# Two cross-attentions in one kernel: the image outputs of each pair's first batch move from TensorE to GpSimd, and a batch's text outputs are transposed through one PSUM tile

## The chip, the cores and the metric

The kernel runs on one core of a Trainium2 chip. The metric is the device time of one execution in microseconds (us). The engines that matter here are TensorE (matrix products and transposes, results in PSUM), VectorE, ScalarE, GpSimd and SyncE, whose queue issues nearly all of the DMAs. In the profile's lines they are called PE, DVE, ACT, POOL and SP; PEld is TensorE's loading of weights, which overlaps its products. Every engine takes its own instructions in order and waits on semaphores for the others. [...]

## The reference

Two cross-attention layers run one after the other on x (64 batches of 256 tokens and 320 channels, float32), both with 20 heads of 16 channels. Layer 0 attends to 77 context tokens (its image part is empty here). Layer 1 splits the context into 73 text tokens and 4 image tokens. What matters here is layer 1, per batch and head:

```
probs_t  = softmax(q . k_t * scale)                   # 256 x 73
text_out = probs_t . v_t
sem      = cosine(probs_t . text, image tokens)       # 256 x 4
probs_ip = softmax(q . k_ip * scale + 0.5 * sem) * spatial_mask
out      = (text_out + probs_ip . v_ip) @ W_out + b_out + x
```

The last product of the fourth line's weights, `probs_ip . v_ip`, has a contraction over only 4 image tokens for each head. This product, for 16 of the 20 heads and for one of the two batches of a pair, is what the change moves.

## The kernel before

**Pairs and steps.** Two batches form a pair p (32 pairs). A pair takes ten steps, numbered k = 0 to 9, and the main loop counts steps g = 10 p + k. In each step, layer 0 handles one unit (a batch's 128 tokens by 8 heads, as scores of 4 row groups by 2 heads) and layer 1 handles one unit of an earlier pair, 13 steps behind (`LAG`). Work that belongs to whole batches or pairs (queries, keys, values, projections, image attention) is spread over the steps by `fillers(k, p)`, which returns four lists: `first`, `second`, `third` and `begin`. Each list is run at a fixed place in the step, so the list decides where an operation stands in every engine's order.

**A step on the engines.** At its start, TensorE writes the layer-1 weighted sums of the unit before (L760, L766) and the scores of both layers (L646) into one PSUM tile `sc` of four banks. There is one such tile (`psc`, bufs=1), so the next step's L760 can start only when VectorE has read the scores (L664, L666) and the products (L777, L780), and ScalarE has copied the sums out (L1092, in `sums_out`). Before that, `begin` runs, and if `held["i"]` is set, the copies that `image_attend` returned are put on ScalarE's queue. After the scores, TensorE transposes layer 1's probabilities (`transposed(1)`: `tr` and `rtr`, L710 and L711), does the `first` fillers, transposes layer 0's probabilities, and then does `second`, `attend` and `third`. ScalarE copies the transposes to SBUF (L717, L718 for layer 1, L736, L737 for layer 0), exponentiates (L674, L677, L678) and evacuates the fillers. GpSimd normalizes layer 0's probabilities (`normalize`, tile `parts`, L697), which the next step's transposes need, and then does the GpSimd work of the fillers. A manual dependency (`keep_order`) holds the order of TensorE, ScalarE, VectorE and GpSimd as it was written down; SyncE's DMAs are in that order only in the beginning and are ordered by the scheduler after that.

**Buffers.** Tiles with the same tag share their buffers: a new tile of a tag with bufs=1 may be written only when the last reader of the tile before has finished. PSUM has two banks for transposes (`ptr`, tag `tr`) and two for all other fillers (`pms`, tag `ms`). A filler such as `value_rows` (L381, the projection of context rows to values; L382 is its copy) takes one `ms` bank and thus waits for the copy of what lay in it.

**The text and image path of layer 1, pair p-2 while pair p is at its steps.** `text_output` divides the sums by the softmax's denominator on GpSimd (`an` for 16 heads, `an_last` for the last 4 heads); it runs when a batch's last unit ends, in step 9 for the first batch (b = 0) and in step 4 for the second (b = 1). `text_transposed` turns `an` on TensorE in four transposes (L846), through two `tr` tiles, into `aT` (two copies L848): in step 0 for b = 0, in step 5 for b = 1. The image weights (`image_scores` to `image_weights`, tile `iw`) are ready on GpSimd at the start of steps 2 (b = 0) and 7 (b = 1). For the 16 heads, `image_transposed` turns the weights of both batches on TensorE in step 7 (four transposes L948, one copy L950), and `image_attend` multiplies them in step 8 with block-diagonal image values `vip` (four products L960: both batches, two halves of the channels) into two `ms` tiles `ipv`. ScalarE copies these into `ip_out` (two copies L970) and GpSimd adds `ip_out` to `aT` (L972). `vip` is loaded with 16 small DMAs a batch (`image_values`, L478) and masked on GpSimd in step 9 (`place_image_values`, L483). The last 4 heads were already done on GpSimd before the change: `last_image_outputs` multiplies and adds for each of the 4 image tokens (tile `ip_last`, L857, and `an_last`, L860), in step 4 for b = 0 and in step 7's `second` list for b = 1; its values `vlast` are one broadcast DMA a batch (L489). In step 8, `last_transposed` transposes `an_last` (L866), and in step 9 `project` does the output projection from `aT`.

For the last pair, `image_attend` adds from PSUM on VectorE instead of copying with ScalarE.

## Time and profile before

| what | value |
|---|---|
| time, median of 3 runs (range) | 2574.57 us (2571.29 to 2574.81) |
| the profiled execution's own time | 2574.26 us |
| its span in the profile | 2572.5 us, granted TensorE clock 0.997 |
| busy: PE, PEld, DVE, ACT, POOL | 2514.1, 2009.7, 1952.3, 1506.8, 1654.6 us |
| HBM traffic | 95.56 MB read, 33.91 MB written |
| `vip` loads (L478) | 1024 DMAs of 4.0 KB |
| `vlast` loads (L489) | 64 DMAs of 128.0 KB |
| a usual pair in the middle (timeline of PE) | 75.9 us for ten steps |
| the steps 0 to 9 of such a pair | 8.0, 7.7, 7.65, 9.3, 8.6, 6.4, 6.8, 6.9, 6.75, 7.8 us |

The profile's span leaves out 1.8 us of the profiled execution's own time. A step is counted here from the start of its L760 to the start of the next step's L760 in TensorE's timeline. The lengths repeat from pair to pair within a few hundredths of a microsecond, apart from six pairs in which one more block of value rows lengthens steps 6 and 8 to 8.6 and 8.9 us. The engines' busy shares are averages over steps that differ in what limits them, so the stages around the change have to be read in the timeline. In a timeline line, the first number is the start in us, the second the time until the merged group ends, and a bracket at the end gives the idle time of the engine before it and the instruction that released it. In the view by stretches, PEclk is the granted clock of TensorE as a share of full speed.

### The profile page before, as it was taken

Reading aid. Unit: us, or ns where it says so; the run is one execution under the profiler, and the core shown is the slowest. Engines: PE = TensorE matmul, PEld = TensorE weight load, DVE = VectorE, ACT = ScalarE, POOL = GpSimd, SP = SyncE. Lnnn points to the kernel's source line nnn. Section 1 sums busy time; section 2 is a strip of 40 time slices with the busy share of each in tenths; the row PEclk is TensorE's granted clock in tenths of the full one; section 3 lists DMA queues with packets and bytes.
Section 4 is the critical chain, followed back from the end, with each engine's and each line's share of the span. In section 5 each row is a group of like instructions: output and inputs, shape, how many; then the busy total and the mean of one; then the engine's idle time right before and its main releaser. Section 6 shows DMA issues by size and latency. Waiting matters only on the chain.

```text
span 2572.5 us, 74528 instructions
## 1 busy us (share of the span) xinstructions
PE 2514.1 (98%) x27178; PEld 2009.7 (78%) x27178; DVE 1952.3 (76%) x3609; ACT 1506.8 (59%) x3893; POOL 1654.6 (64%) x4026
## 2 busy tenths in 40 slices
PE   7999999999999999999999999999999999999998
PEld 6677878777787777788777787778787777787776
DVE  4578777878777778777877777877877777777764
ACT  3465665665665665666656566666566666566543
POOL 3466666676666676666666666666666666666653
PEclk9999999999999999999999999999999999999999
DMA  5212211121211121211121211121211121211000
GB/s 166 59 44 62 60 48 43 54 59 56 63 46 48 49 59 55 64 45 52 45 60 54 64 44 53 45 59 54 66 45 50 44 60 54 64 41 42 25 25 27
DMA packets 186405, 138.33 MB, mean 54 GB/s; under 512 B 81016, under 2 KB 164728, under 8 KB 186040
## 3 DMA queue, kind: packets, MB, share of 16 engines
q1 hardware_dynamic: 185176, 132.41, 18.1%
q8 instruction: 217, 3.56, 0.6%
q14 instruction: 148, 1.21, 0.2%
q10 hardware_dynamic: 864, 1.15, 0.1%
HBM read 95.56 MB, written 33.91 MB: 50 GB/s over the span
## 4 chain that ended last, share of the span: by engine, by line
PE 72%; DVE 15%; ACT 5%; DMA 2%; issue 2%; SPq 2%; POOL 2%; DVEq 0%; POOLq 0%; ACTq 0%
PE sc L760 11%; PE tr L710 9%; PE q_ps L537 8%; PE sc L646 6%; DVE w L666 5%; PE o_ps L537 4%; PE v_ps L381 4%; PE sc L766 4%; PE k_ps L336 4%; DVE mx L664 4%; PE pv L794 3%; PE q_ps L546 3%; DVE prod L777 2%; PE pv L799 2%; PE o_ps L621 2%
## 5 line engine op out<-in xcount | busy, mean ns | idle before, releaser
L664 DVE TENSOR_REDUCE mx<-sc 128x8 f32<-128x584 f32 (+1 forms) x640 | 495.4, 774 | 423.9 <-PE sc L646 423.8
L697 POOL TENSOR_TENSOR parts<-w,sm 128x512 f32<-128x512 f32 (+1 forms) x640 | 440.5, 710 | 371.1 <-DVE sm L693 165.7
L666 DVE TENSOR_TENSOR w<-sc,mx 128x616 f32<-128x616 f32 x640 | 511.8, 800 | 66.7 <-ACT kT L339 0.5
L710 PE MATMUL tr<-ident,parts 128*128 128x128 f32 x2560 | 408.6, 282 | 8.2 <-POOL parts L697 3.8
L717 ACT COPY pt<-tr 128x512 f32<-128x512 f32 x320 | 187.5, 586 | 341.7 <-PE tr L710 339.0
L760 PEld LDWEIGHTS sc<-gv,pt 64*128 64x128 f32 x5120 | 319.5, 187 | 77.0 <-ACT sums L1092 53.7
L710 PEld LDWEIGHTS tr<-ident,parts 128*128 128x128 f32 x2560 | 285.0, 141 | 116.2 <-issue 76.1
L760 PE MATMUL sc<-gv,pt 64*128 64x94 f32 x5120 | 353.1, 277 | 15.8 <-ACT sums L1092 10.7
L674 ACT ACTIVATE w<-w 128x616 f32<-128x616 f32 x320 | 231.0, 722 | 151.9 <-DVE w L666 143.0
L692 DVE TENSOR_REDUCE sm<-w 128x8 f32<-128x616 f32 x320 | 250.7, 784 | 13.9 <-ACT w L674 13.9
L646 PE MATMUL sc<-kbd,q 32*128 32x154 f32 x5120 | 248.1, 305 | 1.0 <-ACT q L591 1.0
L537 PE MATMUL q_ps<-x,wq 128*128 128x256 f32 x1024 | 232.4, 379 | 3.4 <-ACT kT L339 3.4
L537 PE MATMUL o_ps<-aT,wo 128*128 128x256 f32 x1024 | 232.7, 380 | 0.0
L1092 ACT COPY sums<-sc 128x168 f32<-128x168 f32 x320 | 96.5, 302 | 230.8 <-DVE prod L780 230.1
L1174 DVE TENSOR_REDUCE nrm<-prod 128x8 f32<-128x584 f32 x320 | 227.0, 709 | 0.4
L777 DVE TENSOR_TENSOR prod<-sc,parts 128x512 f32<-128x512 f32 x320 | 217.7, 680 | 4.0 <-PE sc L766 4.0
L537 PEld LDWEIGHTS q_ps<-x,wq 128*128 128x128 f32 x1024 | 189.3, 190 | 27.6 <-ACT kT L339 4.6
L537 PEld LDWEIGHTS o_ps<-aT,wo 128*128 128x128 f32 x1024 | 190.4, 191 | 23.5 <-issue 0.2
L677 ACT ACTIVATE parts<-w 128x512 f32<-128x512 f32 x320 | 207.8, 649 | 0.0
L646 PEld LDWEIGHTS sc<-kbd,q 32*128 32x128 f32 x5120 | 186.5, 186 | 5.9 <-issue 4.8
L736 ACT COPY pt<-tr 128x512 f32<-128x512 f32 x256 | 150.4, 587 | 62.6 <-PE tr L710 62.6
L381 PE MATMUL v_ps<-wv,cf 128*128 128x320 f32 (+1 forms) x624 | 182.1, 438 | 0.0
(147 smaller groups left out, 4791.0 us busy)
## 6 DMA issues: line engine op xcount, KB each, us to landing
vip<-vip_rows SPq DMA_DIRECT2D x1024, 4.0 KB
out_dram<-x SPq DMA_DIRECT2D x64, 256.0 KB
x<-in_x_dram SPq DMA_DIRECT2D x31, 512.0 KB
v_rows<-vs SPq DMA_DIRECT2D x38, 320.0 KB
vm<-v_rows SPq DMA_DIRECT2D x152, 80.0 KB
ct<-in_ctx_dram SPq DMA_DIRECT2D x32, 308.0 KB
cf<-in_ctx_dram SPq DMA_DIRECT2D x38, 256.0 KB
g_rest<-gram_rest SPq DMA_DIRECT2D x512, 0.5 KB
```

Source lines behind the costliest of these rows:

```text
L381: nc.tensor.matmul(ps[:n, :C], cfs[i][:, k, :n], wv[l][:, k, :], start=(k == 0), stop=(k == KE - 1))
L537: nc.tensor.matmul(ps[b][:, m, :], w[:, k, m * P : (m + 1) * P], main[:, k, b * S : (b + 1) * S], start=(k == 0 and m == 0), stop=False,)
L646: nc.tensor.matmul(ps[:, r, 2 * T * l : 2 * T * (l + 1)], q[rows, b, :] if part == 2 else q[rows, t0 : t0 + P], kbd[rows, part].rearrange( ...
L664: nc.vector.tensor_reduce(mx, sc[:, :, :, :nt], AX.X, ALU.max)
L666: nc.vector.tensor_tensor(w, sc, mx.unsqueeze(3).broadcast_to([P, 4, 2, T]), ALU.subtract)
L674: nc.scalar.activation(w, w, AF.Exp, scale=SCALE)
L692: nc.vector.tensor_reduce(sm, w, AX.X, ALU.add)
L697: nc.gpsimd.tensor_tensor(two[:, 8 * t0 : 8 * t1].rearrange("p (h t) -> p h t", h=8), w[:, :, t0:t1], sm.unsqueeze(2).broadcast_to([P, 8, ...
L710: nc.tensor.transpose(ps[:, i, :], flat[:, i * P : (i + 1) * P], ident)
L760: nc.tensor.matmul(ps[:, i % 2 * 2 + j, at : at + GV], pt[half_rows, i, :], gv[b][half_rows, part, i, :], start=start and i < 2, stop=False,)
L777: nc.vector.tensor_tensor(prod[:, :, :, :M], sm[:, :, :, :M], w[:, :4].rearrange("p (e a) j t -> p (a j) e t", e=2), ALU.mult)
L1174: nc.vector.tensor_reduce(eight(stats[q, b][2], u), prod, AX.X, ALU.add)
```

## The change

For the first batch of each pair (b = 0), the 16 heads' image outputs are no longer made on TensorE. `head_values` loads the 4 image tokens' values once, broadcast to 128 partitions (tile `vt`, 512 KB, one DMA). `head_products` multiplies them by the weights for one image token (128x512), and `head_sum` adds the result to `an[0]`; four of each are spread over GpSimd's steps 2 to 4. `image_values`, `place_image_values`, `image_transposed` and `image_attend` then handle only b = 1: two transposes and two products where there were four, and the GpSimd add covers 128x512 instead of 128x1024. `vip` is loaded in step 9 and masked in step 1 of the following pair's steps.

`text_transposed` uses one `tr` tile and one copy for a batch. Since `an[0]` now has to hold the image outputs first, b = 0 is transposed in step 6 (`second` list) instead of step 0, after b = 1, and `an` has two buffers. In step 6 the sums are copied out (`sums_out`) after layer 0's transposes are copied instead of before. `last_image_outputs` for b = 0 is split: two tokens in step 4 and two in step 5, where the load of b = 1's `vlast` follows.

All products of this kind (`head_products`, `last_image_outputs`) and the copy out of `ipv` now share the tag `ip_out`, which has one buffer; before, `last_image_outputs` had a tile of its own (`ip_last`). `iw`, `vip` and `iwT` become smaller or lose a buffer.

```diff
--- before.py
+++ after.py
@@ -469,11 +469,17 @@
             rest0[:n].rearrange("p (i g) -> p i g", g=4).unsqueeze(3).broadcast_to([n, 2, 4, D]), ALU.mult,
         )
 
+    def head_values(p):
+
+        r0 = 2 * p * NIP
+        v = vips[p, "heads"] = small.tile([P, NIP, 2 * P], F32, tag="vt", name=f"vt{p}", bufs=1)
+        nc.sync.dma_start(v, vip_rows[r0 : r0 + NIP, : 2 * P].unsqueeze(0).broadcast_to([P, NIP, 2 * P]))
+
     def image_values(p, b):
 
 
         n, r0 = HT * NIP, (2 * p + b) * NIP
-        vip = vips[p, b] = big.tile([n, 2 * P], F32, tag="vip", name=f"vip{p}_{b}", bufs=3)
+        vip = vips[p, b] = big.tile([n, 2 * P], F32, tag="vip", name=f"vip{p}_{b}", bufs=1)
         for h in range(HT):
             nc.sync.dma_start(vip[h * NIP : (h + 1) * NIP, :], vip_rows[r0 : r0 + NIP, : 2 * P])
 
@@ -827,33 +833,47 @@
         sums = stats[p, b][1]
         rec = small.tile([P, 2 * H], F32, tag="rec", name=f"rec{p}_{b}", bufs=2)
         nc.vector.reciprocal(rec, sums[:, :, NIP + D])
-        an = big.tile([P, 2, HT, D], F32, tag="an", name=f"an{p}_{b}", bufs=1)
+        an = big.tile([P, 2, HT, D], F32, tag="an", name=f"an{p}_{b}", bufs=2)
         if b == 0:
             lasts[p] = big.tile([P, 2, 2, H - HT, D], F32, tag="an_last", name=f"an_last{p}", bufs=1)
         by_head(an, lasts[p][:, :, b], sums[:, :, NIP : NIP + D], rec)
-        return an
+        ans[b] = an
+
+    ans = {}
+
+    def head_products(p, t):
+
+        full = [P, 2, HT, D]
+        prod = made["ip"] = big.tile(full, F32, tag="ip_out", name=f"ip{p}_{t}", bufs=1)
+        nc.gpsimd.tensor_tensor(
+            prod, vips[p, "heads"][:, t].rearrange("p (h d) -> p h d", d=D).unsqueeze(1).broadcast_to(full),
+            weights[p, 0][:, :, :, t].unsqueeze(3).broadcast_to(full), ALU.mult,
+        )
+
+    def head_sum():
+
+        nc.gpsimd.tensor_add(ans[0], ans[0], made["ip"])
 
     def text_transposed(p, b):
 
-        an = made["an"]
-        if b == 0:
+        an = ans[b]
+        if b == 1:
             aTs[1, p] = channels("aT1", f"aT1_{p}", 1)
-        main = aTs[1, p][0]
+        ps = ptr.tile([P, 2, 2, P], F32, tag="tr", name=f"atr{p}_{b}")
         for s in range(2):
-            ps = ptr.tile([P, 4, P], F32, tag="tr", name=f"atr{p}_{b}{s}")
             t = an[:, s].rearrange("p h d -> p (h d)")
             for i in range(2):
-                nc.tensor.transpose(ps[:, i, :], t[:, i * P : (i + 1) * P], ident)
-            t0 = b * S + s * P
-            nc.scalar.copy(main[:, :, t0 : t0 + P], ps[:, :2])
-
-    def last_image_outputs(p, b):
+                nc.tensor.transpose(ps[:, i, s, :], t[:, i * P : (i + 1) * P], ident)
+        nc.scalar.copy(aTs[1, p][0][:, :, b * S : (b + 1) * S], ps.rearrange("p i s t -> p i (s t)"))
+
+    def last_image_outputs(p, b, tokens=range(NIP)):
 
         v = vips[p, b, "last"].rearrange("p t (h d) -> p t h d", d=D)
         w, to = weights[p, b, "last"], lasts[p][:, :, b]
         part = [P, 2, H - HT, D]
-        for t in range(NIP):
-            prod = small.tile(part, F32, tag="ip_last", name=f"ip_last{p}_{b}{t}", bufs=1)
+        for t in tokens:
+            prod = big.tile([P, 2 * S], F32, tag="ip_out", name=f"ip_last{p}_{b}{t}", bufs=1)
+            prod = prod[:, : 2 * HALF].rearrange("p (s h d) -> p s h d", s=2, d=D)
             nc.gpsimd.tensor_tensor(
                 prod, v[:, t].unsqueeze(1).broadcast_to(part), w[:, :, :, t].unsqueeze(3).broadcast_to(part), ALU.mult
             )
@@ -931,7 +951,7 @@
         nc.vector.tensor_reduce(r, num, AX.X, ALU.add)
         nc.vector.reciprocal(r, r)
         nc.gpsimd.tensor_mul(m, m, smask.unsqueeze(2).broadcast_to([P, 2, H]))
-        to = weights[p, b] = small.tile([P, 2, HT, NIP], F32, tag="iw", name=f"iw{p}_{b}", bufs=2)
+        to = weights[p, b] = small.tile([P, 2, HT, NIP], F32, tag="iw", name=f"iw{p}_{b}", bufs=1)
         last = weights[p, b, "last"] = small.tile(
             [P, 2, H - HT, NIP], F32, tag="iw_last", name=f"iw_last{p}_{b}", bufs=1
         )
@@ -942,36 +962,31 @@
     def image_transposed(p):
         n = HT * NIP
         ps = ptr.tile([P, 4, P], F32, tag="tr", name=f"itr{p}")
-        for b in range(2):
-            w = weights[p, b].rearrange("p s h t -> p s (h t)")
-            for s in range(2):
-                nc.tensor.transpose(ps[:n, 2 * b + s, :], w[:, s], ident)
-        wT = big.tile([n, S2], F32, tag="iwT", name=f"iwT{p}", bufs=1)
-        nc.scalar.copy(wT, ps[:n].rearrange("p j t -> p (j t)"))
+        w = weights[p, 1].rearrange("p s h t -> p s (h t)")
+        for s in range(2):
+            nc.tensor.transpose(ps[:n, s, :], w[:, s], ident)
+        wT = big.tile([n, S], F32, tag="iwT", name=f"iwT{p}", bufs=1)
+        nc.scalar.copy(wT, ps[:n, :2].rearrange("p s t -> p (s t)"))
         return wT
 
     def image_attend(p):
 
         wT = made["wT"]
-        both = [pms.tile([P, 512], F32, tag="ms", name=f"ipv{p}_{i}") for i in range(2)]
-        for b in range(2):
-            for i in range(2):
-                rows = slice(i * QR, (i + 1) * QR)
-                nc.tensor.matmul(
-                    both[i][:, b * S : (b + 1) * S], vips[p, b][rows, i * P : (i + 1) * P],
-                    wT[rows, b * S : (b + 1) * S], start=True, stop=True,
-                )
+        both = [pms.tile([P, 512], F32, tag="ms", name=f"ipv{p}_{i}")[:, :S] for i in range(2)]
+        for i in range(2):
+            rows = slice(i * QR, (i + 1) * QR)
+            nc.tensor.matmul(both[i], vips[p, 1][rows, i * P : (i + 1) * P], wT[rows, :], start=True, stop=True)
 
         def out_of(i):
-            main = aTs[1, p][0]
+            main = aTs[1, p][0][:, :, S:]
             if p == NP - 1:
-                nc.vector.tensor_add(main[:, i, :], both[i], main[:, i, :])
+                nc.vector.tensor_add(main[:, i], both[i], main[:, i])
                 return
             nc.scalar.copy(t[:, i, :], both[i])
             if i:
                 nc.gpsimd.tensor_add(main, t, main)
 
-        t = big.tile([P, 2, S2], F32, tag="ip_out", name=f"ip_out{p}", bufs=1)
+        t = big.tile([P, 2, S], F32, tag="ip_out", name=f"ip_out{p}", bufs=1)
         return [lambda i=i: out_of(i) for i in range(2)]
 
 
@@ -993,7 +1008,6 @@
                 add(1, p, values, 0, p, 0)
             add(0, p - 1, gram, p - 1, 0)
             add(0, p - 3, project_last, 1, p - 3)
-            add(2, p - 2, text_transposed, p - 2, 0)
             if p:
                 add(2, p, place_values, 0, p, 0)
             add(2, p - 1, values, 1, p - 1, 0)
@@ -1004,7 +1018,9 @@
                 add(1, p, place_values, 0, p, 0)
             add(0, p - 1, project, 0, p - 1)
             add(1, p - 2, last_image_values, p - 2, 0)
+            add(1, p - 2, head_values, p - 2)
             add(1, p - 1, place_gram, 0)
+            add(2, p - 2, place_image_values, p - 2, 1)
             add(1, p, keys_by_head, 0, p, 1)
             add(1, p - 1, keys_by_head, 1, p - 1, 0)
         elif k == 2:
@@ -1017,6 +1033,7 @@
             add(2, p - 1, lambda: made["q"]())
             add(1, p - 1, place_values, 1, p - 1, 0)
             add(1, p, values, 0, p, 1)
+            add(2, p - 2, head_products, p - 2, 1)
         elif k == 3:
             add(0, p + 1, load_context, p + 1)
             add(0, p, lambda: last_queries(0, p)())
@@ -1025,13 +1042,18 @@
             add(1, p - 1, queries, 1, p - 1)
             add(1, p, place_values, 0, p, 1)
             add(1, p - 1, keys_by_head, 1, p - 1, 1)
+            add(1, p - 2, head_sum)
+            add(1, p - 2, head_products, p - 2, 2)
+            add(1, p - 2, head_sum)
+            add(1, p - 2, head_products, p - 2, 3)
         elif k == 4:
             if p == 0:
                 add(0, p, image_keys, 1)
             else:
                 add(0, p, keys, 1, p, 0)
             add(1, p - 1, values, 1, p - 1, 1)
-            add(1, p - 2, last_image_outputs, p - 2, 0)
+            add(1, p - 2, head_sum)
+            add(1, p - 2, last_image_outputs, p - 2, 0, range(2))
             add(1, p + 1, queries, 0, p + 1)
         elif k == 5:
             if p == 0:
@@ -1039,7 +1061,8 @@
             add(0, p + 1, keys, 0, p + 1, 0)
             add(1, p - 1, gram, p - 1, 1)
             add(2, p - 2, text_transposed, p - 2, 1)
-            add(1, p - 2, last_image_values, p - 2, 1)
+            add(2, p - 2, last_image_outputs, p - 2, 0, range(2, NIP))
+            add(2, p - 2, last_image_values, p - 2, 1)
         elif k == 6:
             while len(made_rows) * P < min(NB, 2 * (p + 2)) * T:
                 rows_todo.extend((len(made_rows), l) for l in range(2))
@@ -1051,12 +1074,12 @@
             else:
                 add(1, p, keys, 1, p, 1)
             add(1, p, place_image_keys, p)
+            add(2, p - 2, text_transposed, p - 2, 0)
         elif k == 7:
             add(0, p + 1, keys, 0, p + 1, 1)
             add(1, p + 1, last_keys, p + 1)
             add(1, p - 2, lambda: made.update(wT=image_transposed(p - 2)))
             add(1, p - 2, last_image_outputs, p - 2, 1)
-            add(1, p - 1, image_values, p - 1, 0)
             if p == 0:
                 add(1, p, image_rows)
         elif k == 8:
@@ -1064,15 +1087,13 @@
                 add(0, p, value_rows, *rows_todo.pop(0))
             add(1, p - 1, place_gram, 1)
             add(1, p + 1, keys_by_head, 0, p + 1, 0)
-            add(1, p - 1, image_values, p - 1, 1)
             add(1, p - 1, place_values, 1, p - 1, 1)
             add(1, p - 2, last_transposed, p - 2)
             add(3, p - 2, lambda: held.update(i=lambda: image_attend(p - 2)))
         else:
             add(0, p - 2, project, 1, p - 2)
             add(1, p + 1, values, 0, p + 1, 0)
-            for b in range(2):
-                add(1, p - 1, place_image_values, p - 1, b)
+            add(1, p - 1, image_values, p - 1, 1)
         return f
 
     rows_todo, made_rows = [], [0, 1]
@@ -1148,7 +1169,7 @@
         if k != 2:
             for fn, args in first:
                 fn(*args)
-        if before1 and k in (1, 6, 8):
+        if before1 and k in (1, 8):
             sums_out(ps)
         if last0:
             transposed(0, *last0)
@@ -1161,7 +1182,7 @@
             keep_busy(8)
         if now[0] and k == 5:
             exponential(0, g, *now[0])
-        if before1 and k not in (1, 6, 8):
+        if before1 and k not in (1, 8):
             sums_out(ps)
         if now[1]:
             exponential(1, g, *now[1])
@@ -1174,11 +1195,13 @@
             nc.vector.tensor_reduce(eight(stats[q, b][2], u), prod, AX.X, ALU.add)
             if ends:
                 image_squares(q, b)
-                made["an"] = text_output(q, b)
+                text_output(q, b)
                 later[g + 1] = [(image_scores, (q, b))]
                 middle[g + 2] = (image_shifted, (q, b))
                 later[g + 2] = [(image_exponential, (q, b))]
                 early[g + 3] = [(image_weights, (q, b))]
+                if b == 0:
+                    early[g + 3] += [(head_products, (q, 0)), (head_sum, ())]
         for fn, args in second:
             fn(*args)
         if last0:
```

## The prediction

> **What bounds the kernel now.** I read the page first, then TensorE's timeline for step lengths, then the step that changes most (step 8) engine by engine, and last the view by stretches for the granted clock.

> ```profile
> span 2572.5 us, 74528 instructions
> PE 2514.1 (98%) x27178; PEld 2009.7 (78%) x27178; DVE 1952.3 (76%) x3609; ACT 1506.8 (59%) x3893; POOL 1654.6 (64%) x4026
> ```

> TensorE has almost no idle time, GpSimd has a third of its time free. That invites moving work from the one to the other, but averages do not tell what ends step 8. This is TensorE in step 8 of a usual pair (start 1281.05, next step 1287.80):

> ```profile
> 1281.05 1.13 PE L760 MATMUL sc<-gv,pt 64*128 64x94 f32 x16
> 1282.97 1.03 PE L960 MATMUL ipv<-iwT,vip 32*128 32x256 f32 x8
> 1283.93 0.66 PE L710 MATMUL tr<-ident,parts 128*128 128x128 f32 x4
> 1284.66 2.42 PE L381 MATMUL v_ps<-wv,cf 128*128 128x320 f32 x8
> 1286.92 0.60 PE L710 MATMUL tr<-ident,parts 128*128 128x128 f32 x4
> 1287.80 0.46 PE L760 MATMUL sc<-gv,pt 64*128 64x94 f32 x4
> ```

> ScalarE (first three lines) and GpSimd (last three) in the same step:

> ```profile
> 1284.03 1.07 ACT L970 COPY ip_out<-ipv 128x512 f32<-128x512 f32 x2 [1.39 <-PE ipv L960]
> 1287.12 0.43 ACT L382 COPY vs<-v_ps 128x320 f32<-128x320 f32 x1 [0.75 <-PE v_ps L381]
> 1287.45 0.30 ACT L1092 COPY sums<-sc 128x168 f32<-128x168 f32 x1
> ...
> 1281.39 1.38 POOL L697 TENSOR_TENSOR parts<-w,sm 128x512 f32<-128x512 f32 x2 [1.57 <-ACT parts L678]
> 1286.29 0.46 POOL L860 TENSOR_TENSOR an_last<-an_last,ip_last 128x128 f32<-128x128 f32 x1
> 1286.70 2.37 POOL L972 TENSOR_TENSOR aT<-ip_out,aT 128x1024 f32<-128x1024 f32 x1
> ```

> The reader should see a chain: the first ipv copy (start 2.98 us into the step) frees a PSUM bank, v_ps starts at 3.61, ends near 6.0, its copy L382 and the sums behind it on ScalarE end at 6.70, and the next step starts at 6.75. The view of line L970 confirms the first link:

> ```profile
> L970 ACT COPY ip_out<-ipv x62: 586/590/595, 210.0 to 2508.1; 128x512 f32<-128x512 f32 x62
>   PEld v_ps L381: 6.1, 29
> ```

> In 29 pairs v_ps waits for that copy already. Meanwhile GpSimd is still busy with the last four heads of b = 1: its last add ends 5.70 us into step 8, and I find 5.69 to 6.00 in all these 29 pairs.

> **The change part by part.** Times are for one pair, line numbers are of the kernel before.

> *The new wait (step 8).* The products of `last_image_outputs` for b = 1 and the tile that ScalarE copies ipv into now share one `ip_out` buffer. So the first ipv copy has to wait until GpSimd's last L860 has read its product. GpSimd cannot be earlier: its work in step 8 starts behind `parts` (L697), which waits for VectorE's sums of step 7. Step 7 gets shorter by 0.26 (below), so the last add ends 5.96 into step 8; with 0.02 of hand-over the copy starts at 5.98 instead of 2.98. It is shorter: 128x256, for which the copy L818 takes 0.37 where L970 takes 0.59. v_ps then starts at 5.98 + 0.37 + 0.04 = 6.39 instead of 3.61, 2.78 later. Behind the waiting copy on ScalarE's queue stand the second ipv copy, both copies of layer 1's transposes, layer 0's exponential, L382 and the sums; TensorE waits for the bank (v_ps) and then for the sums. All that follows v_ps keeps its distance, 3.18 to the next step, so step 8 grows by 2.78 to 9.5 us. The 0.43 us that half of ipv saves (four of eight records, 0.85 in the chain of waits) falls into this wait and is worth nothing.

> *Step 7, two transposes fewer.* Four L948 take 0.51 in the chain of waits, so 0.25 to 0.26 go. TensorE ends step 7 (sums are ready 0.44 before), so this counts in full: -0.26.

> *Steps 0 and 6, the text of b = 0.* Four transposes L846 take 0.59 in the chain. Step 0 is ended by TensorE, with the sums ready 0.8 earlier (1226.97 against 1227.78): -0.57. Step 6 now ends with TensorE waiting for the sums: the last filler's products are through at about 1273.7, the next L760 starts at 1274.17. So of 0.63 (with a gap) only some 0.15 shows: +0.15. In the six pairs whose step 6 carries one more block of value rows there is no such slack: +0.6. Copying the sums after layer 0's transposes costs nothing: those transposes end at 1272.84, their two copies take 0.86, and VectorE's product that releases the sums ends at 1273.78. If they came later, at most that 0.86 would be added.

> *GpSimd's new work.* A 128x512 product with a broadcast operand takes 1.05 (L697). For the add, the rows are 0.457 for 128x128 (L860) and 2.367 for 128x1024 (L972); their straight line gives 1.27 for 128x512. Four of each are 9.3 us, plus 0.08 between dependent ones, 9.9; with half of L972 for the add (1.18) it is 9.5, with twice L884's 0.63 for 128x256 for the product 10.8. One mask L483 (0.62) and half of L972 (1.1) go. Net +8 us of 76, GpSimd busy about 1900 us. Its cover is the idle time in steps 2 to 5: 4.43 before `least` (L897, step 4) takes four operations (4.7 us from 1254.5 to 1259.4, so L897 is about 0.5 late, and VectorE's L901 starts only at 1260.13 anyway); 2.14 before L921 in step 6 takes two tokens of `last_image_outputs` (2.0). `parts` of step 2 is late by 0.5 and of step 4 by 0.3, but the transposes that read them start 2.1 and 3.6 after `parts` ends now. So nothing; if each operation took twice as long, `parts` of step 4 would be 5.0 late and 1.4 us a pair would show.

> *Queues.* SyncE issues 16 small loads fewer, at 0.33 each (three in 0.97), and one 512 KB load more. This one waits for the last product of the pair before (step 4); behind it are the context load for a later pair and `gram`'s copies, which are ready only in step 5, so its wait delays nothing. Its data are first read some 60 us later. `vlast` of b = 1 is issued after the second split half, about 10 us before it is read. In step 3 the value loads stood behind up to fifteen `vip` loads, and four pairs lost 0.2 to 3.0 us in step 4 behind late values (4.4 in all): between 0 and -4.4, I take -2.

> *Sum with a full clock.* 2.78 - 0.26 - 0.57 + 0.15 = 2.10 in 23 pairs, 2.55 in six: 48.3 + 15.3 = 63.6. The last pairs have no v_ps; they gain a little (fewer transposes, shorter copies, some -1). Together 63.6 - 1 - 2 = +61, on the profiled execution's 2574.3 (0.3 below the median): 2635 us.

> *The clock.* TensorE would stand idle for 3.1 us in step 8, from 3.2 to 6.39, after the sparse score products. The trace shows what this can do. Here one idle time of 1.39 us (2412.0 to 2413.4) lies in the first stretch, and the last two lines are around one of 2.72 us (1950.15 to 1952.87), before and after which there are dense 128x128 products:

> ```profile
> 2411.70:2415.10 3.40, 2.02 (x39) 1.00 0.00 0
> 2415.10:2418.50 3.40, 2.65 (x21) 0.50 0.00 0
> 2418.50:2421.90 3.40, 3.40 (x28) 0.50 0.04 9
> 2421.90:2425.30 3.40, 3.40 (x52) 0.99 0.15 34
> ...
> 1950.90:1954.30 3.40, 1.43 (x7) 1.00 0.26 64
> 1954.30:1957.70 3.40, 3.40 (x52) 1.00 0.12 25
> ```

> After the short idle the clock was 0.50 for two stretches of 3.4 us and that step took 9.95 where others take 6.42: 1.75 lost per stretch. After 1.60 us at 2490 one stretch was at 0.50, after 3.31 at 2553 two. Five others in the trace (1.49 to 2.72) left it at 1.00. An idle time of 3.1 among sparse products is nearest to those that dropped, and what follows at half speed (v_ps) ends the step. I take one such stretch, 1.7 us, in three pairs of four: 29 x 0.75 x 1.7 = +37, bounds 0 and two stretches nearly everywhere (+89). So 2635 + 37 = 2672, rounded to 2670.

> [...]

> **The rivals.**
> - *The wait isn't there or is met in time.* It decides if GpSimd's last L860 ended by 2.6 us into step 8 instead of 5.96. Then step 8 loses some 0.2 (the sums end 6.5 into it), a usual pair -0.26 - 0.57 + 0.15 - 0.2 = -0.88, six pairs -0.43: -23, with the ends and loads 2548. For it: idle GpSimd elsewhere. Against it: its order is fixed and 5.69 is the earliest of the 29 ends.
> - *The wait, but the clock holds.* 2635, up to 2655 where few pairs drop. For it: 2.72 idle at 1.00. Against it: 1.39 idle dropping.
> - *The wait, and two slow stretches in most pairs.* 2635 + 89 = 2724. For it: two of three drops lasted two stretches. Against it: v_ps and the projection of step 9 are dense and should bring the clock back after one.
> - *GpSimd becomes the bound in steps 2 to 5.* Only with operations twice as long: +1.4 x 29 = +41 more. No row of GpSimd's elementwise work is so slow; I leave it to the tail.

> **How the numbers follow.** Wait with dropped clock, 2655 to 2708: 0.58. Wait with a clock that mostly holds, 2628 to 2655: 0.24. Above 2708: 0.08. Faster: 0.08. Within 0.2% (5 us, what a measurement of this kernel can tell from no change): 0.02. The range 2628 to 2708 holds 0.82. Slower is 0.58 + 0.24 + 0.08 = 0.90.

> **What would show it.** In the profile after: the first ipv copy idles some 3.4 us longer per pair for GpSimd's `an_last` add, about 90 us in sum; v_ps is preceded by 3.1 us of TensorE idle; step 8 takes 9.5 us or more and steps 7 and 0 about 6.6 and 7.45; step 6 stays near 6.95. GpSimd near 1900 us busy, ScalarE about 30 less than before. The clock row shows stretches at 0.50 around step 8, or the mean stays at 1.00, which decides between 2635 and more. The prediction is wrong if the ipv copy starts near 3 us into step 8, or if `parts` comes after the transposes that read it in steps 3 to 5.

## The result, and the profile after

| | time, median (range), us | span, us | granted clock |
|---|---|---|---|
| before (with the runs beside the changed kernel) | 2573.2 (2571.29 to 2574.81) | 2572.5 | 0.997 |
| changed | 2686.34 (2682.82 to 2689.27) | 2687.5 | 0.976 |

The changed kernel takes 1.0439 of the time before, 95% interval [1.0426, 1.0451]: it is 113 us slower. The prediction said 2670 (2628 to 2708), 96 us above the profiled execution of the kernel before.

The first fence shows lines of the page of the changed kernel: the engines' busy time, the chain that ended last, and the group of v_ps products (busy time and mean ns of one, then idle time before them and its releaser). Its last line is the same group in the page of the kernel before.

```profile
span 2687.5 us, 73637 instructions
PE 2535.9 (94%) x26986; PEld 2021.2 (75%) x26986; DVE 1959.1 (73%) x3609; ACT 1485.1 (55%) x3829; POOL 1893.8 (70%) x4250
...
PE 61%; DVE 12%; POOL 10%; ACT 5%; DMA 5%; issue 4%; SPq 3%; DVEq 0%; POOLq 0%; ACTq 0%
...
L381 PE MATMUL v_ps<-wv,cf 128*128 128x320 f32 (+1 forms) x624 | 220.4, 509 | 89.4 <-ACT ip_out L985 89.4
...
L381 PE MATMUL v_ps<-wv,cf 128*128 128x320 f32 (+1 forms) x624 | 182.1, 438 | 0.0
```

TensorE has fewer instructions than before and is busy for longer: 2535.9 against 2514.1 us. The v_ps group shows both reasons in one line. It now has 89.4 us of idle time in front of it (before: none), and the same 624 products take 220.4 us (before: 182.1), because some of them run at a lower clock (0.59 in one stretch of the second fence below). GpSimd's share of the chain that ends last was 2% and is 10%.

Step 8 of a usual pair (start 2068.81, next step 2079.87) in the timeline of TensorE, ScalarE and GpSimd:

```profile
2068.81 1.13 PE L766 MATMUL sc<-gv,pt 64*128 64x94 f32 x16
2070.72 0.60 PE L978 MATMUL ipv<-iwT,vip 32*128 32x256 f32 x4
2075.10 4.06 PE L381 MATMUL v_ps<-wv,cf 128*128 128x320 f32 x8 [3.08 <-ACT ip_out L985]
2078.99 0.60 PE L716 MATMUL tr<-ident,parts 128*128 128x128 f32 x4
...
2074.67 0.65 ACT L985 COPY ip_out<-ipv 128x256 f32<-128x256 f32 x2 [4.33 <-POOL an_last L880]
2075.21 0.60 ACT L723 COPY pt<-tr 128x512 f32<-128x512 f32 x1
...
2074.19 0.45 POOL L880 TENSOR_TENSOR an_last<-an_last,ip_last 128x128 f32<-128x128 f32 x1
2075.40 1.27 POOL L987 TENSOR_TENSOR aT<-ip_out,aT 128x512 f32<-128x512 f32 x1 [0.76 <-ACT ip_out L985]
```

The products ipv end at 2071.3, but their copy starts only at 2074.67, when GpSimd's last `an_last` add (L880, which has read the last product in the shared buffer) is through. TensorE then stands idle for 3.08 us, and its eight v_ps products take 4.06 us where 2.42 is normal. The view by stretches around the same place (stretch, its length, busy time of PE, PEld, DVE, ACT, POOL, then PEclk, DMA share, GB/s) says why:

```profile
2068.80:2071.90 3.10, 3.10 (x53) 2.55 (x49) 1.75 (x5) 1.49 (x6) 2.44 (x5) 1.00 0.13 30
2071.90:2075.10 3.20, 0.12 (x3) 0.00 (x1) 2.98 (x5) 0.43 (x2) 2.35 (x6) 0.99 0.00 0
2075.10:2079.20 4.10, 4.10 (x10) 2.72 (x11) 1.62 (x3) 1.50 (x5) 2.79 (x5) 0.59 0.16 38
2079.20:2083.00 3.80, 3.80 (x55) 3.31 (x54) 0.87 (x2) 2.59 (x8) 3.67 (x13) 1.00 0.48 160
```

The clock falls from 0.99 to 0.59 behind the idle time, in the stretch in which the work that ends the step is being done, and is at 1.00 in the next. In the view of waits (total us, number of times, longest) the new wait and a second loss can be read:

```profile
ACT ip_out L985 <- POOL an_last L880: 134.4, 31, 4.7
...
PE v_ps L381 <- ACT ip_out L985: 89.4, 29, 3.1
...
ACT nrm L925 <- DVE nrm L921: 13.9, 7, 2.7
...
PE k_ps L336 <- ACT q L597: 10.3, 6, 2.2
```

The last two are not among the waits that the profile of before lists. They belong to step 5, which became long in six pairs. In step lengths (means from TensorE's timeline, in us; a row runs from step 5 of a pair to step 4 of the next, and the means are over rows 2 to 28, counted from 0, which are called pairs below):

| step | 5 | 6 | 7 | 8 | 9 | 0 | 1 | 2 | 3 | 4 |
|---|---|---|---|---|---|---|---|---|---|---|
| before | 6.42 | 7.21 | 6.88 | 7.23 | 7.82 | 7.99 | 7.69 | 7.65 | 9.29 | 8.74 |
| changed | 7.12 | 7.33 | 6.73 | 11.45 | 7.82 | 7.27 | 7.69 | 7.61 | 9.29 | 8.67 |

Over 29 pairs these differences make 122 us in step 8, 20 in step 5, 3.5 in step 6, and -21 in step 0, -4 in step 7, -3 in steps 2 and 4: 117 us, for spans that differ by 115.

### The profile page after: what moved, and what is told of

Same layout as the page of the kernel before. It is cut to its first block, busy times and chain, and to the rows that moved or that the text cites. A ratio compares the mean times of both kernels' runs of the same rounds, so it can differ in the third digit from the quotient of the medians.

```text
span 2687.5 us, 73637 instructions
## 1 busy us (share of the span) xinstructions
PE 2535.9 (94%) x26986; PEld 2021.2 (75%) x26986; DVE 1959.1 (73%) x3609; ACT 1485.1 (55%) x3829; POOL 1893.8 (70%) x4250
## 3 DMA queue, kind: packets, MB, share of 16 engines
q14 instruction: 144, 1.18, 0.2%
## 4 chain that ended last, share of the span: by engine, by line
PE 61%; DVE 12%; POOL 10%; ACT 5%; DMA 5%; issue 4%; SPq 3%; DVEq 0%; POOLq 0%; ACTq 0%
PE sc L766 9%; PE v_ps L381 8%; PE tr L716 7%; PE q_ps L543 7%; PE sc L652 5%; PE o_ps L543 4%; DVE w L672 4%; PE k_ps L336 3%; DVE mx L670 3%; PE sc L772 3%; POOL an_last L880 2%; PE q_ps L552 2%; POOL ip_last L877 2%; PE pv L800 2%; DVE prod L783 2%
## 5 line engine op out<-in xcount | busy, mean ns | idle before, releaser
L723 ACT COPY pt<-tr 128x512 f32<-128x512 f32 x320 | 187.6, 586 | 358.0 <-PE tr L716 356.4
L381 PE MATMUL v_ps<-wv,cf 128*128 128x320 f32 (+1 forms) x624 | 220.4, 509 | 89.4 <-ACT ip_out L985 89.4
L381 PEld LDWEIGHTS v_ps<-wv,cf 128*128 128x128 f32 (+1 forms) x624 | 131.8, 220 | 150.9 <-ACT ip_out L985 96.3
```

The costliest lines, as they stand in the source:

```text
L381: nc.tensor.matmul(ps[:n, :C], cfs[i][:, k, :n], wv[l][:, k, :], start=(k == 0), stop=(k == KE - 1))
```

## The experiments

Two theories stood against each other at first. One: the shared buffer makes ScalarE's copy wait, and that wait with the clock behind it is the whole of step 8. The other: GpSimd has too much work, and the buffer only shows it. All ratios below are against the kernel before, run beside the experiment.

| run | time, us | ratio to before, 95% |
|---|---|---|
| own_tile | 2554.83 | 0.9923 [0.9907, 0.9940] |
| lend_before | 2682.56 | 1.0422 [1.0402, 1.0442] |
| fill_wait | 2648.82 | 1.0292 [1.0276, 1.0307] |
| lend_two | 2577.75 | 1.0020 [1.0011, 1.0030] |
| lend_three | 2639.19 | 1.0252 [1.0235, 1.0269] |
| early_products | 2589.54 | 1.0059 [1.0038, 1.0080] |
| own_heads_first | 2541.72 | 0.9873 [0.9858, 0.9887] |
| one_more_product | 2570.18 | 0.9989 [0.9980, 0.9999] |
| least_on_vector | 2599.71 | 1.0103 [1.0086, 1.0120] |
| one_more_least | 2600.34 | 1.0104 [1.0088, 1.0119] |
| least_late | 2543.26 | 0.9881 [0.9864, 0.9897] |
| two_banks | 2540.08 | 0.9869 [0.9855, 0.9884] |

### The buffer taken out of the change, and put alone into the kernel before

own_tile, an edit of the changed kernel:

```diff
-            prod = big.tile([P, 2 * S], F32, tag="ip_out", name=f"ip_last{p}_{b}{t}", bufs=1)
-            prod = prod[:, : 2 * HALF].rearrange("p (s h d) -> p s h d", s=2, d=D)
+            prod = small.tile(part, F32, tag="ip_last", name=f"ip_last{p}_{b}{t}", bufs=1)
```

> The changed kernel, only that the products of the last heads have a small tile of their own again (ip_last, 128x128) instead of the buffer that the copy of ipv waits for. Theory (the shared buffer): the copy ipv starts some 3.0 us into step 8 again, v_ps at about 3.6, no half-speed stretch there, step 8 about 6.5 instead of 11.4 on average: 29 x 4.9 = 142 us less, about 2545, of which the longer step 5 of six pairs (about 19 us above the step's usual length) may or may not be part: 2540 to 2562, faster than before by 0.4% or more. Rival 1 (GpSimd's added work is the cause, the buffer only shows it): step 8 stays above 8.5 and the time above 2630. Rival 2 (the wait goes elsewhere: the add to aT, the next transposes or the load of vt is late next): step 8 is 6.5, another step takes at least 1 us more in most pairs, 2575 to 2610.

lend_before, an edit of the kernel before:

```diff
-            prod = small.tile(part, F32, tag="ip_last", name=f"ip_last{p}_{b}{t}", bufs=1)
+            prod = big.tile([P, 2 * S2], F32, tag="ip_out", name=f"ip_last{p}_{b}{t}", bufs=1)[:, : 2 * HALF].rearrange("p (s h d) -> p s h d", s=2, d=D)
```

> The kernel before, only that the products of the last heads are made in the buffer ip_out, as the changed kernel has it; no other work is moved. Theory (the shared buffer alone makes the loss): the copy ipv waits for the last sum of GpSimd, v_ps starts about 2.8 us later, step 8 grows from 6.9 to 9.4 with the clock held and to 11 to 12 with one or two half-speed stretches: 2573 + 29 x (2.6 to 5) = 2648 to 2718, about 2690. Rival (the buffer costs only because GpSimd carries the head products too): under 2610.

With its own tile, the changed kernel takes 2554.83 us, 131.5 less than with the shared buffer and 0.8% less than the kernel before. Its step 8 in the timeline of TensorE, ScalarE and GpSimd:

```profile
1969.17 0.60 PE L978 MATMUL ipv<-iwT,vip 32*128 32x256 f32 x4
1970.30 2.34 PE L381 MATMUL v_ps<-wv,cf 128*128 128x320 f32 x8
...
1973.85 1.13 PE L766 MATMUL sc<-gv,pt 64*128 64x94 f32 x16 [0.26 <-ACT sums L1113]
...
1969.79 0.65 ACT L985 COPY ip_out<-ipv 128x256 f32<-128x256 f32 x2 [1.01 <-PE ipv L978]
...
1972.64 0.46 POOL L880 TENSOR_TENSOR an_last<-an_last,ip_last 128x128 f32<-128x128 f32 x1
1973.06 1.27 POOL L987 TENSOR_TENSOR aT<-ip_out,aT 128x512 f32<-128x512 f32 x1
```

GpSimd ends its last add 5.85 us into the step, as late as before the edit (5.83). The copy does not care any more: it starts at 2.54, v_ps follows at 3.05 without idle time, and step 8 takes 6.59 us in a usual pair. So GpSimd's load is not what makes step 8 long.

The kernel before with nothing but the shared buffer takes 2682.56 us, nearly as much as the changed kernel, though none of the new GpSimd work is in it. Its waits:

```profile
ACT ip_out L970 <- POOL an_last L860: 124.6, 30, 4.7
...
PE v_ps L381 <- ACT ip_out L970: 79.0, 29, 3.0
```

Both runs came out within their theory's numbers. The buffer alone accounts for the loss in step 8, in either kernel. This is shown by putting it in and by taking it out.

### The wait without the half clock

fill_wait, an edit of the changed kernel in `transposed`; the added transposes write columns that nothing reads:

```diff
         nc.tensor.transpose(pr[:n, 0, :], flat[:, 4 * P : 4 * P + n], ident)
+        if l and now[0] and g % NU == 8:
+            for i in range(22):
+                nc.tensor.transpose(pr[:, 1 + i % 3, :], ident, ident)
```

> The changed kernel with the wait left in, but 22 more transposes of the identity behind the transposes of step 8, into columns of their bank that nothing reads, so that TensorE works about 3 us of the wait. Theory (the wait itself is some 2.8 us and the rest of step 8 is the halved clock): v_ps starts where it did, lasts 2.4 instead of 4.06, step 8 is 9.4 to 9.6 in all pairs, granted clock back near 0.995, time 2686 - 29 x 2.0 = about 2628 (2615 to 2640). Rival (the lengthening behind the wait is the queue of ScalarE, which makes its copies late whatever the clock): step 8 stays at 11 or above and the time within 2670 to 2690.

The page's group of v_ps for this run:

```profile
L381 PE MATMUL v_ps<-wv,cf 128*128 128x320 f32 (+1 forms) x624 | 182.1, 438 | 20.3 <-ACT ip_out L988 20.3
```

The products are back at 182.1 us in sum and 438 ns each, exactly the values of the kernel before, and step 8 is 9.45 us in every usual pair. That is the prediction's step 8 with a full clock (9.5). Doing useless work on TensorE for 2.4 us a pair (89.4 less 20.3 us of idle time, over 29 pairs) makes the kernel 37.5 us faster: with these transposes in the wait, the clock stays at 1.00 in step 8 of all 29 pairs, and its mean is 0.995 instead of 0.976. The time of 2648.8 lies above the expected 2615 to 2640: the expectation took 2.0 us a pair for the clock, and the step means give 1.52 (11.45 against 9.93, means over all pairs). So the loss in step 8 is two thirds wait, one third clock. The rival, a queue on ScalarE that is late whatever the clock, would have left 2670 or more.

### How long a wait the step bears

In lend_two, only the first two of the second batch's four products use the shared buffer, in lend_three the first three (`n` is 2 or 3):

```diff
-            prod = big.tile([P, 2 * S], F32, tag="ip_out", name=f"ip_last{p}_{b}{t}", bufs=1)
+            pool, tag = (small, "ip_last") if b == 1 and t >= n else (big, "ip_out")
+            prod = pool.tile([P, 2 * S if tag == "ip_out" else 2 * HALF], F32, tag=tag, name=f"ip_last{p}_{b}{t}", bufs=1)
```

> The changed kernel, with a tile of their own for the second batch's last two products in step 7; the first two still use the buffer of the ipv copy. The last sum behind a lent product then ends about 3.8 us into step 8 instead of 5.83, while the ipv matmuls are ready at 2.54: a wait of about 1.25 us. Theory (every us of the wait is one us of step 8, and only a wait of about 3 us brings the half clock): v_ps about 1.25 us later than the 3.05 of the own tile, step 8 7.8, 2555 + 29 x 1.25 = 2591 (2583 to 2599), clock held. Rival (any new idle time there brings the half clock, as 1.4 us did once in the trace of before): 2591 + 29 x 1.5 = 2635.

> As before, three of the four products lent: the third sum ends about 4.85 us into step 8, a wait of about 2.3 us. Theory with the clock held: step 8 8.9, 2555 + 29 x 2.3 = 2622. With the half clock in most pairs: 2622 + 44 = 2666. Which of the two is left open by what has been run; with the wait of 1.25 us at 2591 and that of 3.3 us at 2686, the run says between which waits the half clock begins.

The pairs counted here are the 28 behind the first one that has v_ps in step 8; a held clock is one that stays at 1.00, the half clock is 0.50.

| products lent | TensorE's idle time before v_ps, us | step 8 with a held clock, us | pairs with the half clock in step 8 | time, us |
|---|---|---|---|---|
| 0 (own_tile) | 0 | 6.59 | 0 of 28 | 2554.8 |
| 2 (lend_two) | 1.04 | 7.38 | 0 of 28 | 2577.8 |
| 3 (lend_three) | 2.07 | 8.42 | 17 of 28 | 2639.2 |
| 4 (changed) | 3.08 | 9.43 | 22 of 28 | 2686.3 |

From two products on, one more product lent (one product and one add on GpSimd, 1.02 us) costs its duration: 7.38, 8.42, 9.43. The first two together cost 0.79, since the step bore a part of it: in own_tile, TensorE waits for the sums at the end of step 8, 0.26 us in the pair shown above. That is why lend_two came out at 2578 instead of 2591. The clock comes on top and in jumps: no pair at 1.04 us idle, 17 of 28 at 2.07. The open question of lend_three is answered in between: 2639 lies between 2622 (held) and 2666 (most pairs dropped).

### The same buffer, the products earlier

early_products, an edit of the changed kernel (list 0 is `first`, list 1 `second`):

```diff
-            add(1, p - 2, last_image_outputs, p - 2, 1)
+            add(0, p - 2, last_image_outputs, p - 2, 1)
```

> The changed kernel with its shared buffer, but the second batch's last image products and sums stand in GpSimd's order right behind their weights in step 7, ahead of the copy of att and of the normalization of the attention, where GpSimd is idle 2.1 us and then 1.6 us. Theory (what counts is when the last sum ends, not the memory): they run from 3.4 into step 7 to about 0.4 into step 8, the ipv copy waits for nothing, the normalization starts at most 0.3 us later: as with the own tile, 2555 (2550 to 2566). Rival 1 (the load of these values is not there so early): the sums end later and the normalization with them, step 8 above 7.5, over 2580. Rival 2 (sharing costs by itself): above 2640.

The theory's 2555 was missed; rival 1 is what happened. The view of waits:

```profile
POOL ip_last L877 <- DMA vlast<-vip_rows: 96.5, 31, 4.7
```

The values' load, issued at the end of step 5, lands 3.1 us later on average than GpSimd now wants it, so the adds still end late and step 8 is 7.6 us in a usual pair. But with the shared buffer left in place, the time falls from 2686 to 2589.5: it is the end of the last reader that counts, not the sharing. A version with an earlier load was not tried.

### Step 5: what stands ahead of a small instruction

own_tile still has the long step 5 (mean 7.05, six pairs of 7.4 to 10.5). In the changed kernel it looks like this in one of these pairs, in the timeline of GpSimd, VectorE, ScalarE and TensorE:

```profile
825.62 0.72 POOL L455 TENSOR_TENSOR v<-vm,half 128x320 f32<-128x320 f32 x1 [4.14 <-DMA vm<-v_rows]
828.30 1.28 POOL L855 TENSOR_TENSOR an<-an,ip 128x512 f32<-128x512 f32 x1
829.66 1.10 POOL L848 TENSOR_TENSOR ip<-vt,iw 128x512 f32<-128x512 f32 x1
830.84 1.27 POOL L855 TENSOR_TENSOR an<-an,ip 128x512 f32<-128x512 f32 x1
832.19 1.12 POOL L848 TENSOR_TENSOR ip<-vt,iw 128x512 f32<-128x512 f32 x1
833.24 0.28 POOL L917 TENSOR_TENSOR least<-sums 128x40 f32<-128x40 f32 x1
...
833.56 0.20 DVE L921 SCALAR_TENSOR_TENSOR nrm<-least,nrm 128x40 f32<-128x40 f32 x1 [3.82 <-POOL least L917]
...
833.79 0.24 ACT L925 ACTIVATE nrm<-nrm 128x40 f32<-128x40 f32 x1 [2.69 <-DVE nrm L921]
...
836.07 2.42 PE L336 MATMUL k_ps<-ct,wk 128*128 128x154 f32 x8 [2.18 <-ACT q L597]
```

The context values `vm` come 4.14 us late. Behind them in GpSimd's order stand four new head instructions, and behind those `least`, 0.28 us long. The norm on VectorE, the square root on ScalarE, the query copies behind it and at last TensorE's k_ps wait for it, one after the other; k_ps then runs at half speed (2.42 us for what takes 1.22; the granted clock is 0.50 in these 2.42 us). The late values were there before the change as well (18.5 us in seven waits, 19.9 after it), but the idle time behind them was free to catch up. This is the same pair on GpSimd in the kernel before:

```profile
796.21 0.72 POOL L455 TENSOR_TENSOR v<-vm,half 128x320 f32<-128x320 f32 x1 [3.83 <-DMA vm<-v_rows]
799.77 0.27 POOL L897 TENSOR_TENSOR least<-sums 128x40 f32<-128x40 f32 x1 [0.84 <-ACT sums L1092]
```

The values are 3.83 us late, and GpSimd still has 0.84 us to spare ahead of `least`. The six pairs with a long step 5 in the changed kernel are the six in which these values come more than 2 us late there, and in none of them GpSimd has any idle time left ahead of `least`.

own_heads_first is own_tile with the placing of these values behind the head instructions, in step 3:

```diff
-            add(1, p, place_values, 0, p, 1)
             add(1, p - 1, keys_by_head, 1, p - 1, 1)
             add(1, p - 2, head_sum)
             add(1, p - 2, head_products, p - 2, 2)
             add(1, p - 2, head_sum)
             add(1, p - 2, head_products, p - 2, 3)
+            add(1, p, place_values, 0, p, 1)
```

> The own tile as above, and in step 3 the placing of the second batch's values (GpSimd, which waits for their load) stands behind the products and sums of the heads instead of ahead of them. Theory (where these values come late, the four head instructions stand behind that wait and make the minimum, the norm and the queries of step 5 late): the lengthened step 5 of about six pairs (10.2 to 11.7 instead of 6.4) is gone, 10 to 19 us below the kernel with the own tile alone. Rival 1 (the late load itself makes step 5 late, and the order does nothing): within 4 us of the own tile alone. Rival 2 (placing comes too late for the value products of the next steps, or the next load starts later): slower than the own tile alone by 10 us or more.

2541.72 us, 13.1 below own_tile and 1.3% below the kernel before. Step 5 is 6.47 in nearly all pairs (mean 6.58). GpSimd's wait for the values falls from seven times to two, since it does the head work in that time (own_tile first, then own_heads_first):

```profile
POOL v L455 <- DMA vm<-v_rows: 20.1, 7, 4.3
...
POOL v L455 <- DMA vm<-v_rows: 3.3, 2, 3.0
...
PE k_ps L336 <- ACT q L597: 2.4, 4, 1.4
```

How little room is left behind it was measured by making one head product twice in step 2 (same output):

```diff
             add(2, p - 2, head_products, p - 2, 1)
+            add(2, p - 2, head_products, p - 2, 1)
```

> The own tile and the head instructions first, with one head product of step 2 made twice: 1.1 us more GpSimd work in each pair, the same output. Theory (in steps 2 to 4 GpSimd runs without idle time in this kernel, its square least ends just as ScalarE wants the norm, and so all further work there is paid in step 5): step 5 from 6.47 to about 7.5, 2541.7 + 29 x 1.05 = 2572 (2562 to 2590, the upper end with a half-speed stretch in some pairs). Rival (GpSimd's work is hidden in its idle time, as the prediction costs it): 2542, at most 2547.

2570.18 us: 1.11 us more GpSimd work costs 28.5 us in all, 0.87 a pair in step 5 (25 us in 29 pairs) and the rest at the two ends of the kernel, though GpSimd is busy only 75% of the span. The waits of the run:

```profile
ACT nrm L925 <- DVE nrm L921: 39.8, 30, 2.1
DVE nrm L921 <- POOL least L917: 38.4, 62, 1.7
...
PE k_ps L336 <- ACT q L597: 22.4, 29, 1.6
```

The third wait now occurs 29 times and takes 22.4 us; with the product made once it was 2.4 us in four. So in own_heads_first GpSimd is full from step 2 to `least` (in a usual pair its timeline has 0.9 us of idle time in these 23.9 us, in gaps under 0.1 us), and 75% is an average over steps that do not have this limit.

Three runs moved `least` itself. least_on_vector (on own_tile) and one_more_least (on one_more_product) make it on VectorE at the same place of the order:

```diff
-        nc.gpsimd.tensor_mul(t, total, total)
+        nc.vector.tensor_mul(t, total, total)
```

> The own tile, the head instructions where the change put them, and the minimum's square (least, 128x40, 0.27 us) on VectorE instead of GpSimd. Theory (the long step 5 comes because least stands on GpSimd behind the late values and the head instructions, and the norm, its table load and the query copies of ScalarE and k_ps of TensorE follow it): the step 5 of 10.4 us in some six pairs is 6.4 again, 2554.8 - 13 = 2542 (2536 to 2546), as with the head instructions first. Rival 1 (something else on GpSimd in that queue holds the end, the normalization of the attention say): within 4 us of 2555. Rival 2 (VectorE now waits in order for the copy of sums and is late with the next normalization in every pair): over 2560.

> The same doubled product, with least on VectorE. Theory (least is the only thing in those steps through which GpSimd's work reaches the end): step 5 back at 6.4 to 6.5, 2538 to 2546. Rival (the placed values or the normalization behind them on GpSimd are next in line): 2555 or more.

2599.71 and 2600.34 us. The long step 5 is indeed gone (most of the six long pairs are at 7.2), and the second product now costs under 0.1 us in step 5 (7.13 against 7.05, though the two runs also differ in where the values are placed). But VectorE, too, works in order here, and there `least` waits 1.50 us for ScalarE's copy of the sums, with the normalization queued behind it:

```profile
1157.61 0.24 DVE L917 TENSOR_TENSOR least<-sums 128x40 f32<-128x40 f32 x1 [1.50 <-ACT sums L1113]
1157.77 0.79 DVE L698 TENSOR_REDUCE sm<-w 128x8 f32<-128x616 f32 x1
```

Step 0 grows from 7.27 to 8.6 and step 5 to 7.0: the theory and its second rival were both right, and the rival was larger. The theory of one_more_least missed its time (2538 to 2546) for this reason too; its rival's "2555 or more" came true, but by VectorE's queue and not by GpSimd's. least_late (on own_tile) puts it further back on VectorE:

```diff
-        nc.gpsimd.tensor_mul(t, total, total)
+        nc.vector.tensor_mul(t, total, total)
...
-        if ends:
-            image_least(*before1[:2])
...
+                image_least(q, b)
                 image_squares(q, b)
```

> The own tile, the head instructions where the change put them, least on VectorE but behind the sum for the norm, right ahead of the instruction that uses it, so that VectorE waits for no copy. Theory (least's place on GpSimd is what makes step 5 long, and the losses of the last run but two are VectorE's wait for the copy of sums, 1.5 us before step 0 and 0.4 us before step 5): no step 5 above 7.3, step 0 back from 8.6 to 7.3 or 7.6 (the 0.24 to 0.67 us of least itself now stand in the chain of the norm), 2542 plus 29 x (0 to 0.9) = 2542 to 2568. Rival (the loss is least's own time on VectorE): step 0 stays near 8.6 and the time near 2600.

2543.26 us: step 0 is 7.27 again, no step 5 of pairs 2 to 28 is above 7.2, and the head instructions stand where the change had put them. Two independent edits, one on what stands ahead of `least` and one on `least` itself, thus remove about the same loss, 11.6 and 13.1 us.

### One bank for the text

two_banks is own_heads_first with the transposes and copies of `text_transposed` as they were before the change, at the new places:

```diff
-        ps = ptr.tile([P, 2, 2, P], F32, tag="tr", name=f"atr{p}_{b}")
         for s in range(2):
+            ps = ptr.tile([P, 4, P], F32, tag="tr", name=f"atr{p}_{b}{s}")
...
+            nc.scalar.copy(aTs[1, p][0][:, :, t0 : t0 + P], ps[:, :2])
-        nc.scalar.copy(aTs[1, p][0][:, :, b * S : (b + 1) * S], ps.rearrange("p i s t -> p i (s t)"))
```

> The own tile and the head instructions first, but a batch's text transposed in two banks with two copies of 128x256, as before the change, at the new places (first batch in step 6, second in step 5). Theory (one bank spares a copy's start-up on ScalarE and a bank of the two that transposes share, both beside TensorE's work): steps 5 and 6 within 0.15 us, 2541.7 plus 0 to 6. Rival (the second bank holds up the transposes of the attention in step 6, where TensorE has no idle time): step 6 grows by 0.3 us or more, 2550 or above.

2540.08 us, no step differs by more than 0.03 us in the mean. The single bank of the change's second half is thus worth nothing measurable (ScalarE is busy 1494.8 us instead of 1489.8, beside TensorE's work).

## Why the prediction was right, and where not

- **The new wait in step 8: right.** It gave the copy's start at 5.98 us into the step, v_ps at 6.39 and 3.1 us of idle time; the medians are 5.86 and 6.29, and 3.08. A pair with a held clock takes 9.43 (predicted 9.5), which is 2.68 longer than before (predicted 2.78), 78 us in 29 pairs. The 0.1 is the step 7 that shortened less than predicted (below): the last add ends 5.83 us into step 8 instead of 5.96. fill_wait, lend_before and own_tile show the mechanism from three sides.
- **The clock: right in kind, 37 us taken where some 40 came.** The half clock came in 22 of 28 pairs. Three in four were assumed, from no row that gives a share; in the traces of the last section, where an idle time lies on a grid of 3.413 us separates the pairs that lost the clock from those that kept it, so the near agreement is luck. The step means of the changed kernel and fill_wait differ by 44 us over 29 pairs, their profiled spans by 41, their times by 37.5. One stretch costs 1.69 us (11.12 less 9.43; 1.7 taken), and six usual pairs had two: 12.2 to 12.35 us. The rival with a held clock (2635) and the one with two slow stretches nearly everywhere (2724) are both out.
- **GpSimd's new work: wrong, the term that failed.** "So nothing" costed it against the idle time before `least` in a usual pair. In some of the pairs that idle time is already spent: the values come late, and they stand ahead of the new instructions in GpSimd's order. Six pairs lost 19 to 20 us in step 5. The late loads were in the trace of before and were used for the queue's term only. The doubling of durations, named as the condition for trouble, was not needed; the order was enough. GpSimd's durations themselves were right (1.11 and 1.27 us measured, 1.05 and 1.27 taken), and its 1894 us busy too.
- **Step 0: -0.72 instead of -0.57**, 21 us instead of 16.5. The four transposes were 0.59, as taken. The rest stands in the timeline of before: ScalarE's exponential L674 waited 0.38 us in step 0 for GpSimd's mask of `vip` (L483), which the change moves to step 1; the attention products behind it start 0.17 us earlier after the change. The traces bear this out. In the seven pairs of the kernel before that lack this wait, step 0 takes 7.86 instead of 8.02 us. It also takes 7.86 in all pairs of lend_before behind the first, where the wait does not occur and the transposes are untouched. 7.86 less 7.27 is 0.59, the four transposes.
- **Step 6: 0.04 in usual pairs and 0.43 in the six longer ones** (0.15 and 0.6 taken): 3.5 us instead of 7. **Step 7: -0.15 instead of -0.26**, 4 us instead of 7.5. In the medians of TensorE's timelines the transposes of the image weights take 0.31 us instead of 0.56, as predicted, but start 1.19 instead of 1.10 us after the kl_ps products ahead of them began; what holds them 0.09 us is open.
- **Queues: -2 taken, -2 measured** in step 4 (8.74 to 8.67 in the mean). That the shorter queue did this isn't shown: lend_before, whose loads are those of the kernel before, has 8.60 there.
- **Three readings that were off without harm.** GpSimd's `parts` in step 8 waited for ScalarE's L678, as the line shown says, and not for VectorE's sums. From v_ps to the next step it is 3.14 us, in the lines shown as after the change, not 3.18. The 1.75 us lost per slow stretch also holds an idle time of 0.76 us in that step.

Together the sum was right within 17 us, in part by luck, since errors of both signs cancel (here a minus is time that the prediction lacked): step 5 (-20) and the clock (-4 to -7) missing, step 0 (+4.5) and step 6 (+3.5) better than taken, step 8's wait (+3) and step 7 (-3) nearly even. The rival "the wait isn't there" was priced at 2548; own_tile, which is just that, took 2554.8 with the loss in step 5 and own_heads_first 2541.7 without it. The rest of the change is therefore worth 0.8% as it stands, and 1.3% with the head instructions ahead of the late values; sharing a tile of 512 bytes a partition turned it into a loss of 4.4%.

## What to carry to other kernels

When two tiles come to share a buffer, ask who reads the old tile last, on which engine and when, and who stands behind the new writer; memory saved between two engines can be a wait from one to the other, here 89.4 us of idle time on TensorE. Before work is placed in an engine's idle time, look at the pair (or pass) in which that time is already used, most of all where a wait for a DMA stands ahead of it in the same queue, and at the small instruction behind it that another engine waits for. An idle time of TensorE costs more than its length when the clock falls behind it: here 3.08 us of it made a step 8 of 11.12 us where the clock fell and of 9.43 where it held.
